# Seven products instead of eight for the gate projection of ten token tiles, in a one-core decoder layer

## The chip, the cores and the metric

One core of a Trainium2 chip runs the whole program. The metric is the device time of one execution in microseconds (us); the kernel was timed in three runs, and one further execution was recorded by the hardware profiler. The engines are named as in the profile: PE is TensorE (PEld its weight loads), DVE is VectorE, ACT is ScalarE, POOL is GpSimd, SP is SyncE, which here only issues DMAs.

## The reference

The program computes one decoder layer for x of 16 x 112 tokens by 1024, so 1792 rows. What matters here is its first part:

```python
s = silu(x @ w_gate.T)                     # 1792 x 2752
_, idx = top_k(-abs(s), 1376)              # per row: the 1376 smallest in size
s = s.at[rows, idx].set(0.0)
h = (s * (x @ w_up.T)) @ w_down.T          # 2752 -> 1024
x = layernorm(x + h)
```

Cross attention over a context of 16 x 375 rows (32 heads, 8 key heads), another layer norm and a 4-bit feed-forward layer follow. Everything in the part above is in float32.

## The kernel before

The 1792 rows are 14 tiles of 128 (`TT`), the 1024 inputs are 8 blocks of 128 (`KC`), the 2752 columns (`FF`) are cut in six chunks of 464 or 456 for the gate.

*One stream of matrix work.* `gates_up_keys` makes a queue, `stream`, of steps of TensorE work: the gate projection (`gate_chunk`, 14 tiles x 6 chunks), a step `swap` that closes the space of the gate's weights and opens the up projection's, the up projection (`up_unit`), and the keys and values of the context (`kv_unit`). `emit` takes the next step: it writes the step's matmuls, then the evacuation of the step before it from PSUM (`settle(1)`), then stores that are due (`issue`). Six PSUM banks (`ps_g`) hold products that wait for evacuation.

*A gate chunk* (L180 to L203) is 8 matmuls of 456 or 464 columns into one bank. Its evacuation is a sigmoid on ACT (L199), a multiplication with the bank on DVE (L200) and a store to `s_d` in DRAM by POOL's queue (L201).

*The up projection is already done by Strassen's seven products*, in Winograd's form: tiles are taken in pairs (two rows of blocks), the inputs and the columns in halves, and the columns in four passes (`UPASS`) of 344 (`UW`) out of each half. A unit is one pair in one pass: seven products of 4 matmuls of 344 columns (L297), named "A11 B11", "S2 T2", "A12 B21", "S1 T1", "S4 B22", "S3 T3", "A22 T4". S are sums of blocks of x, made once by POOL during the gate (`sums_of_x`, L175) and kept in DRAM (`xs_d`); T are sums of blocks of weights, made by POOL for each pass (`sum_weights`, L239, four operations). Of the seven evacuations two are copies on ACT (L315, L322), five are additions on DVE, and two results get a further addition on POOL (L325 for c12, L332 for u). Each of the four results is multiplied by the gate's s on POOL (L309) and stored by SP. x and its sums come by `load_first` (L245, L246) and `load_rest` (L252, L253), the weights by `load_weights` (L229).

*The search.* Beside the stream the 1376th smallest |s| of each row is found by bisection on the bits of a float. `load_row` brings a tile's row block from `s_d`, `start` takes the absolute value on ACT (L455), `count` counts the values below a candidate, 1824 columns on ACT (L468) and 928 on DVE (L471), and `update` sets the next candidate on DVE (L479, L480). A tile takes 31 counts. Two tiles run together: the first 16 counts of tile j take turns with the last 15 of tile j - 1. `finish` then queues pieces that build the mask: a count, two comparisons and four scans on DVE (L500, L511, L514, L518), then four pieces on POOL (L531, L532) and a store to `m_d`.

*What sets the order.* The order of instructions on every engine is the order in which the program writes them (`as_written`). The search writes a count, then calls `beside`, which writes one piece of `finish` and as much of the stream as is due:

```python
    share = sum(w for w, _ in list(stream)[:-ends]) / (2 * half * TT)
    def beside():
        nonlocal due
        due += share
        if pieces:
            pieces.popleft()()
        while due > 0 and len(stream) > ends:
            due -= emit()
```

A call of `beside` with the count before it is called a half-step here; there are 448 of them. The stream's steps weigh their columns (a chunk 456 or 464, a product 172, a key unit 285 or 404), so each half-step draws the same weight, 200. Search and stream are thus tied: each position of the search has one position of the stream. The search begins after 13 steps; the last 10 key units are kept for the end.

After this part come the masked products' transposes (between the key units), the down projection (L733), and attention with the last layer (L962 to L1181). They are not touched.

Of the kernel before, what the change touches and what calls it, by code (L numbers as in the profile page):

```python
# [56 lines left out]
LAG = 5  # L57
EARLY = 1
UNPACK = 4
PIECES = 4  # L60


# [44 lines left out]
def gates_up_keys(  # L107
# [50 lines left out]
    xts, acts = {}, {}  # L158

    def load_x(t):  # L160
        xts[t] = room(io, "e", f"xT_{t}", 4 * KH * P, KC, P, bufs=2)
        nc.sync.dma_start(xts[t], xT[t])

    def sums_of_x(j):

        a, b = xts.pop(2 * j), xts[2 * j + 1]
        s = []
        for x, y, op in (
            (b[:, :KH], b[:, KH:], ALU.add), (0, a[:, :KH], ALU.subtract),
            (a[:, :KH], b[:, :KH], ALU.subtract), (a[:, KH:], 1, ALU.subtract),  # L170
        ):
            i = len(s)
            s.append(room(io, "s", f"xs_{j}_{i}", 512, KH, P, bufs=5))
            x, y = (s[z] if isinstance(z, int) else z for z in (x, y))
            nc.gpsimd.tensor_tensor(s[i], x, y, op)  # L175
            nc.gpsimd.dma_start(xs_d[j][:, i], s[i])

    def gate_chunk(t, c):
        off, w = GATE_CHUNKS[c]
        if c == t % 2 and t + 1 < TT:  # L180
            load_x(t + 1)
        if c == 2 and t + 1 == TT:
            load_first(0)
        if c == 2 and t == 2:
            load_weights(0)
        if c == 2 and t == 6:
            sum_weights(0)
# [6 lines left out]
        if c == 0 and t % 2:  # L194
            sums_of_x(t // 2)

        def evacuate():
            s = io.tile([P, 512], F32, tag="s", name=f"s_{t}_{c}", bufs=5)
            nc.scalar.activation(s[:, :w], pg[:, :w], AF.Sigmoid)  # L199
            nc.vector.tensor_mul(s[:, :w], s[:, :w], pg[:, :w])  # L200
            nc.gpsimd.dma_start(s_d[t][:, ds(off, w)], s[:, :w])  # L201

        return evacuate  # L203


    stores = deque()

    def store_later(to, a):
        stores.append((len(stream), to, a))

    def issue(behind=2):
        while stores and stores[0][0] >= len(stream) + behind:
            nc.sync.dma_start(*stores.popleft()[1:])


    pairs = TT // 2
    n_up = UPASS * pairs
    w_up, first, rest, live = {}, {}, {}, {}

    def load_weights(p):  # L220

        if p % 2:
            u = room(upool[0], "w0", f"u0_{p}", 3 * KH * UW, 3, KH, UW)
            v = room(upool[0], "w1", f"u1_{p}", 4 * KH * UW, 4, KH, UW)
        else:
            u = room(lo, "lo0", f"u0_{p}", 5120, 3, KH, UW)
            v = room(lo, "lo1", f"u1_{p}", 5632, 4, KH, UW)
        for to, k, h in ((u[:, 0], 0, 0), (u[:, 2], 0, 1), (v[:, 0], 1, 0), (v[:, 1], 1, 1)):
            nc.sync.dma_start(to, wu[:, ts(k, KH), ds(h * FH + p * UW, UW)])  # L229
        w_up[p] = u, v  # L230

    def sum_weights(p):
        u, v = w_up[p]
        b11, t1, b12, b21, b22, t2, t4 = (
            z.rearrange("p k n -> p (k n)")
            for z in (u[:, 0], u[:, 1], u[:, 2], v[:, 0], v[:, 1], v[:, 2], v[:, 3])
        )
        for to, x, y in ((t1, b12, b11), (t2, b22, t1), (b12, b22, b12), (t4, b21, t2)):
            nc.gpsimd.tensor_tensor(to, x, y, ALU.subtract)  # L239

    def load_first(i):

        j = i % pairs
        a = first[i] = room(io, "e", f"xe_{i}", 4 * KH * P, 4, KH * P, bufs=2)
        nc.sync.dma_start(a[:, :2], xT[2 * j].rearrange("p (h k) n -> p h (k n)", h=2))  # L245
        nc.sync.dma_start(a[:, 2:], xs_d[j].rearrange("p h k n -> p h (k n)")[:, :2])  # L246

    def load_rest(i):

        j = i % pairs  # L250
        a = rest[i] = room(upool[0], "l", f"xl_{i}", 3 * KH * P, 3, KH * P, bufs=2)
        nc.sync.dma_start(a[:, :2], xs_d[j].rearrange("p h k n -> p h (k n)")[:, 2:])  # L252
        nc.sync.dma_start(a[:, 2], xT[2 * j + 1][:, KH:].rearrange("p k n -> p (k n)"))  # L253

    def side_loads(i):
        if i + 1 < n_up:
            load_first(i + 1)
            load_rest(i + 1)
        p, at = divmod(i, pairs)
        if at == (1 if p else 0) and p < UPASS - 1:  # L260
            load_weights(p + 1)
        if at == (4 if p else 2) and p < UPASS - 1:
            sum_weights(p + 1)
        if i == n_up - 4:
            load_keys()


    s_order = [(i, t, h) for i in range(n_up) for t, h in ((0, 0), (0, 1), (1, 0), (1, 1))]
    s_ahead = deque()

    def load_s():
        if s_order:
            i, t, h = s_order.pop(0)
            p, j = divmod(i, pairs)
            s = room(io, "s", f"us_{i}_{t}_{h}", 512, UW, bufs=5)
            nc.sync.dma_start(s, s_d[2 * j + t][:, ds(h * FH + p * UW, UW)])
            s_ahead.append((i, t, h, s))

    def up_unit(i, what):

        p, j = divmod(i, pairs)
        u, v = w_up[p]
        a, b, k = {
            "A11 B11": (first, 0, u[:, 0]), "A12 B21": (first, 1, v[:, 0]),
            "S1 T1": (first, 2, u[:, 1]), "S2 T2": (first, 3, v[:, 2]),
            "S3 T3": (rest, 0, u[:, 2]), "S4 B22": (rest, 1, v[:, 1]),
            "A22 T4": (rest, 2, v[:, 3]),
        }[what]
        st = live.setdefault(i, {})
        if what == "A11 B11":  # L290
            if i == 0:
                for _ in range(4):
                    load_s()
            side_loads(i)
        m = ps_g.tile([P, 512], F32, tag="pg", name=f"pu_{i}_{b}")[:, :UW]
        for n in range(KH):
            nc.tensor.matmul(  # L297
                m, a[i][:, b, ts(n, P)], k[:, n, :], start=(n == 0), stop=(n == KH - 1)
            )

        def own(tag):
            st[tag] = room(upool[0], tag, f"{tag}_{i}", 384, UW, bufs=3 if tag == "u" else 2)
            return st[tag]

        def store(t, h, tag):
            a = st.pop(tag)
            *of, s = s_ahead.popleft()
            assert of == [i, t, h]
            nc.gpsimd.tensor_tensor(a, a, s, ALU.mult)  # L309
            store_later(u_d[2 * j + t][:, ds(h * FH + p * UW, UW)], a)  # L310
            load_s()

        def evacuate():
            if what == "A11 B11":
                nc.scalar.copy(own("c11"), m)  # L315
            elif what == "S2 T2":
                nc.vector.tensor_add(own("u"), st["c11"], m)  # L317
            elif what == "A12 B21":
                nc.vector.tensor_add(st["c11"], st["c11"], m)
                store(0, 0, "c11")  # L320
            elif what == "S1 T1":
                nc.scalar.copy(own("m5"), m)  # L322
            elif what == "S4 B22":
                nc.vector.tensor_add(own("c12"), st["u"], m)
                nc.gpsimd.tensor_tensor(st["c12"], st["c12"], st["m5"], ALU.add)  # L325
                store(0, 1, "c12")
            elif what == "S3 T3":
                nc.vector.tensor_add(st["u"], st["u"], m)
            else:
                nc.vector.tensor_add(own("c21"), st["u"], m)  # L330
                store(1, 0, "c21")
                nc.gpsimd.tensor_tensor(st["u"], st["u"], st.pop("m5"), ALU.add)  # L332
                store(1, 1, "u")

        return evacuate
# [112 lines left out]
    state = {}  # L448

    def load_row(t):  # L450
        acts[t] = rows.tile([P, FF], F32, tag="a", name=f"a_{t}")
        nc.sync.dma_start(acts[t], s_d[t])

# [97 lines left out]
        load_rest(0)  # L551

    stream = deque()
    for t in range(TT):
        for c in range(len(GATE_CHUNKS)):
            stream.append((GATE_CHUNKS[c][1], lambda t=t, c=c: gate_chunk(t, c)))
    stream.append((0, swap))
    for i in range(n_up):
        for what in ("A11 B11", "S2 T2", "A12 B21", "S1 T1", "S4 B22", "S3 T3", "A22 T4"):
# [13 lines left out]
    def emit():  # L573
# [5 lines left out]
            issue()  # L579
        return w  # L580

    load_x(0)

    idle = ps_t.tile([P, 512], F32, tag="pt", name="idle")
# [927 lines left out]
```

## Time and profile before

| what | value |
| --- | --- |
| median of three runs | 2586.28 us (2581.89 to 2591.09) |
| the profiled execution, from first to last instruction | 2587.5 us |
| gate: first matmul to first matmul of the up projection | 6.2 to 528 us |
| up projection | 528 to 987 us |
| keys and values, with transposes | 987 to 1360 us |
| first count of the search, last count | 95.5 to 1312 us |
| mean TensorE clock granted | 0.990 |
| one count on ACT, on DVE | 1.815 us, 1.174 us |
| two passes of a gate matmul of 456 columns | 2 x 0.546 us, pipelined |

The trace records the execution from its first to its last instruction, and no time around it. A float32 matmul is recorded as two passes, so the counts of matmuls in the profile are twice those in the code. Matmuls are pipelined and their ends are modelled: the pace is read from the distance of starts, not from the duration. A bracket behind an instruction gives the idle time of its engine before it and what ended it. Stretches of the span are given in us from its start.

### The profile page before, as it was taken

How to read it: one execution, taken by the hardware profiler on the slowest of the kernel's cores; microseconds unless marked ns; L12 is line 12 of the kernel's file. 1: busy time of each engine (PE TensorE's matmuls, PEld its weight loads, DVE VectorE, ACT ScalarE, POOL GpSimd, SP SyncE). 2: the span in 40 equal slices, each digit the busy share in tenths (PEclk: the TensorE clock that was granted, in tenths of full speed). 3: DMA queues.
4: the chain of work that ended last, by engine and by line, in shares of the span. 5: the costliest groups of instructions: out<-in, count | busy, mean ns of one | idle time of the engine just before them, and what ended most of it. 6: DMA issues, size and time to landing. Idle time of an engine off the chain costs nothing.

```text
span 2587.5 us, 34811 instructions
## 1 busy us (share of the span) xinstructions
PE 2517.6 (97%) x10500; PEld 1527.3 (59%) x10514; DVE 1724.1 (67%) x3636; ACT 1390.3 (54%) x2470; POOL 1203.1 (46%) x1141
## 2 busy tenths in 40 slices
PE   9999999999999999999999999999989999999997
PEld 4444444466666666777764444444666666766663
DVE  0378788878988887677740343247667777777774
ACT  0487787777767776988830000000355555555553
POOL 1113433256457544454250000023478888878873
PEclk9999999999999999999999999999989999999999
DMA  6322332276768677888648223156687878778763
GB/s 244 133 69 87 109 106 76 96 263 231 240 231 278 227 243 268 290 288 292 223 160 289 87 82 112 57 188 225 173 201 184 204 191 202 193 191 193 196 168 110
DMA packets 283609, 478.65 MB, mean 185 GB/s; under 512 B 37856, under 2 KB 208224, under 8 KB 279328
## 3 DMA queue, kind: packets, MB, share of 16 engines
q1 hardware_dynamic: 241184, 374.06, 47.1%
q0 software_dynamic: 27008, 75.76, 9.5%
q10 hardware_dynamic: 15232, 26.62, 3.3%
q8 instruction: 85, 1.39, 0.2%
q14 instruction: 100, 0.82, 0.1%
HBM read 272.12 MB, written 103.50 MB: 145 GB/s over the span
## 4 chain that ended last, share of the span: by engine, by line
PE 49%; DVE 7%; DMA 5%; issue 3%; POOL 3%; ACT 3%; SPq 1%; ACTq 1%; POOLq 0%; DVEq 0%
PE m L733 14%; PE pu L297 7%; PE bank L1124 7%; PE bank L962 5%; PE pk L367 4%; PE pk L375 3%; PE sc L1032 3%; PE po L1087 3%; PE bank L1181 2%; ACT probs L1040 1%; DVE jv L471 1%; PE pt L439 1%; DVE nmax L1038 1%; DMA hm<-m_d 1%; DMA xr<-x_d 1%
## 5 line engine op out<-in xcount | busy, mean ns | idle before, releaser
L468 ACT ACTIVATE ja<-a,cand 128x1824 int8<-128x1824 f32 x434 | 787.9, 1815 | 195.1 <-DVE cand L480 187.0
L471 DVE TENSOR_SCALAR_CACHE_REDUCE jv<-a,cand 128x928 uint8<-128x928 f32 x434 | 509.7, 1174 | 43.6 <-ACT a L455 36.6
L190 PE MATMUL pg<-wg_sb,xT 128*128 128x456 f32 (+1 forms) x1344 | 519.3, 550 | 2.6 <-DMA wg_sb<-in_wg_dram 2.6
L190 PEld LDWEIGHTS pg<-wg_sb,xT 128*128 128x128 f32 x1344 | 255.8, 191 | 265.4 <-issue 257.8
L1040 ACT ACTIVATE probs<-sc,nmax 128x375 f32<-128x375 f32 x512 | 286.4, 572 | 230.7 <-DVE nmax L1038 213.2
L1049 POOL TENSOR_TENSOR probs<-probs,sums 128x1500 f32<-128x1500 f32 x128 | 344.2, 2689 | 129.1 <-DVE sums L1048 107.1
L1038 DVE TENSOR_REDUCE nmax<-sc 128x2 f32<-128x750 f32 x256 | 228.5, 931 | 132.3 <-PE sc L1032 132.2
L297 PE MATMUL pu<-u,xe 128*128 128x344 f32 x896 | 264.1, 453 | 2.3 <-DVE u L317 1.8
L733 PE MATMUL m<-wd,h 128*128 128x512 f32 (+1 forms) x616 | 266.2, 594 | 0.0
L1060 DVE STREAM_TRANSPOSE squares<-probs 128x1536 f32<-128x1536 f32 x128 | 224.1, 1751 | 23.7 <-DMA weights<-squares 13.6
L297 PEld LDWEIGHTS pu<-u,xe 128*128 128x128 f32 x896 | 170.0, 190 | 92.4 <-DVE u L317 2.9
L201 POOL DMA_DIRECT2D s_d<-s x84 | 45.9, 546 | 361.8 <-DVE s L200 298.1
L962 PE MATMUL bank<-x1T,wq_sb 128*128 128x224 f32 x1008 | 211.7, 364 | 0.0
L962 PEld LDWEIGHTS bank<-x1T,wq_sb 128*128 128x128 f32 x1008 | 189.3, 193 | 34.4 <-issue 30.7
L733 PEld LDWEIGHTS m<-wd,h 128*128 128x128 f32 (+1 forms) x616 | 117.2, 191 | 146.8 <-issue 144.8
L297 PE MATMUL pu<-u,xl 128*128 128x344 f32 x672 | 199.5, 453 | 1.9 <-DVE c L330 1.4
L1124 PE MATMUL bank<-wo_sb,aT 128*128 128x256 f32 x832 | 194.8, 388 | 0.0
L955 ACT COPY x1T<-pq 128x448 f32<-128x448 f32 x4 | 1.9, 535 | 349.1 <-DMA sc<-in_qs_dram 333.4
L1124 PEld LDWEIGHTS bank<-wo_sb,aT 128*128 128x128 f32 x832 | 155.3, 191 | 46.4 <-issue 23.8
L1074 POOL DMA_DIRECT2D weights<-squares x320 | 177.7, 561 | 6.9 <-PE po L1087 2.4
L421 POOL TENSOR_TENSOR hs<-hs,hm 128x512 f32<-128x512 f32 (+1 forms) x84 | 97.0, 1163 | 166.8 <-DMA hm<-m_d 148.8
L375 PE MATMUL pk<-wv_sb,ctx 128*128 128x256 f32 (+1 forms) x768 | 173.3, 379 | 0.0
(155 smaller groups left out, 3375.7 us busy)
## 6 DMA issues: line engine op xcount, KB each, us to landing
weights<-squares SPq DMA_DIRECT2D x704, 96.0 KB, 3.3
h<-hT_d SPq DMA_DIRECT2D x56, 640.0 KB, 4.9
weights<-squares POOLq DMA_DIRECT2D x320, 96.0 KB, 3.5
ctx<-in_ctxT_dram SPq DMA_DIRECT2D x16, 1500.0 KB, 8.5
a<-s_d SPq DMA_DIRECT2D x14, 1376.0 KB, 8.2
us<-s_d SPq DMA_DIRECT2D x112, 172.0 KB, 3.8
u_d<-c SPq DMA_DIRECT2D x84, 172.0 KB, 3.1
xe<-in_xT_dram SPq DMA_DIRECT2D x28, 512.0 KB, 5.4
```

The costliest lines, as they stand in the source:

```text
L190: nc.tensor.matmul(pg[:, :w], xts[t][:, kc, :], wg_sb[:, kc, ds(off, w)], start=(kc == 0), stop=(kc == KC - 1),)
L297: nc.tensor.matmul(m, a[i][:, b, ts(n, P)], k[:, n, :], start=(n == 0), stop=(n == KH - 1))
L375: nc.tensor.matmul(pk[:n, :KVD], c[:, kc, ds(at, n)], kv["v"][:, kc, :], start=(kc == 0), stop=(kc == KC - 1),)
L468: nc.scalar.activation(ja, a[:, NV:], AF.Sign, bias=cand, scale=-1.0, accum_out=st["sgn"])
L471: nc.vector.tensor_scalar(jv, a[:, :NV], cand, -(TOPK - 1 - NA / 2), ALU.is_lt, ALU.add, accum_out=st["nlt"])
L733: self.nc.tensor.matmul(bank, a[:r, k, :], b(k)[:r], start=(k == 0), stop=(k == HK - 1),)
L962: nc.tensor.matmul(pq[:, :GT], self.wq_sb[:, kc, ts(mc, P)], self.x1T[g][:, kc, :], start=(kc == 0), stop=(kc == KC - 1),)
L1038: nc.vector.tensor_reduce(nmax[h], sc[h][:, :, :SK], AX.X, ALU.max, negate=True)
L1040: nc.scalar.activation(pr[:, i, :SK], sc[i // 2][:, i % 2, :SK], AF.Exp, bias=nmax[i // 2][:, i % 2 : i % 2 + 1], accum_out=sums[:, i : i ...
L1049: nc.gpsimd.tensor_tensor(pr, pr, sums.unsqueeze(2).to_broadcast([P, 4, SK]), ALU.mult)
L1060: nc.vector.transpose(sq[:, :, n % 2].rearrange("p k (i f) -> p k i f", f=Q), probs[:, n % 3].rearrange("p i (k f) -> p k i f", f=Q),)
L1124: nc.tensor.matmul(pp[:, :256], aT[:, h, r, :], wo_sb[:, h * REP + r, ts(i, 256)], start=(h == 0 and r == 0), stop=(h == 1 and r == REP - 1),)
```

## The change

Tiles 0 to 3 keep the plain gate (24 chunks, `PLAIN = 4`). Tiles 4 to 13, five pairs, get their gate from the units of the up projection, with the gate's weights: the pairs come in two groups, (2, 3) and (4, 5, 6), and each group goes through four column passes. So there are 8 sets of gate weights (4 passes x 2 groups) and 20 gate units, then the 4 sets and 28 units of the up projection as before. Weights of a set are loaded and summed during the set before it.

- A gate unit's four results are not multiplied with s. They are queued (`unsaid`); at the next evacuation `silu` takes their sigmoid on ACT, multiplies on POOL and stores them to `s_d` by SP two steps later.
- x of all tiles is loaded during the first chunks: tiles 2 and 3 in a pair, tiles 4 to 13 at chunk 6 into the space that later holds weights. The sums of x of pairs 2 to 6 are made by POOL beside chunks 8, 10, 11, 12 and 13, of pairs 0 and 1 beside chunks 15 and 20. The first gate weights are loaded at chunk 14, once that space is free again, and summed at 18.
- A tile's row block is loaded for the search only when the tile's last result has been handed to its store (`whole`); until then `load_row` writes further steps of the stream.
- In the up projection, weights are loaded after the fourth product of the set's first unit and summed after the second product of its fourth unit (before: at the start of the second and of the fifth unit; for the first pass, of the first and third).
- `share` follows from the sum of the stream's weights, which is smaller: 192 instead of 200.

```diff
+PLAIN = 4
+GATE_PAIRS = ((2, 3), (4, 5, 6))
...
+    def load_others():
+
+        for tag, size, ts_ in (("lo0", 5120, (4, 5, 6, 7, 12)), ("lo1", 5632, (8, 9, 10, 11, 13))):
+            o = room(lo, tag, f"xo_{tag}", size, len(ts_), KC, P)
+            for i, t in enumerate(ts_):
+                xts[t] = o[:, i]
+                load_x(t)
...
+    beside_plain = {
+        0: lambda: load_x(1), 4: lambda: load_pair(1), 6: load_others, 8: lambda: sums_of_x(2), 10: lambda: sums_of_x(3),
+        11: lambda: sums_of_x(4), 12: lambda: sums_of_x(5), 13: lambda: sums_of_x(6),
+        14: lambda: load_weights(0), 15: lambda: sums_of_x(0), 18: lambda: sum_weights(0),
+        20: lambda: sums_of_x(1), 21: lambda: load_first(0),
+    }
...
+    sets = [(wg, p, js) for js in GATE_PAIRS for p in range(UPASS)]
+    sets += [(wu, p, tuple(range(pairs))) for p in range(UPASS)]
+    units = [(k, j) for k, (_, _, js) in enumerate(sets) for j in js]
...
+    def side_weights(i, b):
+
+        k, j = units[i]
+        if k + 1 == len(sets):
+            return
+        at, n = sets[k][2].index(j), len(sets[k][2])
+        if at == 0 and b == (2 if n < pairs else 3):
+            load_weights(k + 1)
+        if at == (1 if n < pairs else 3) and b == 1:
+            sum_weights(k + 1)
...
+    def silu():
+
+        while unsaid:
+            i, t, h, a = unsaid.popleft()
+            k, j = units[i]
+            g = room(io, "s", f"sg_{i}_{t}_{h}", 512, UW, bufs=5)
+            nc.scalar.activation(g, a, AF.Sigmoid)
+            nc.gpsimd.tensor_tensor(a, a, g, ALU.mult)
+            last = sets[k][1] == UPASS - 1 and (t, h) == (1, 1)
+            store_later(
+                s_d[2 * j + t][:, ds(h * FH + sets[k][1] * UW, UW)], a,
+                (2 * j, 2 * j + 1) if last else (),
+            )
...
         def store(t, h, tag):
             a = st.pop(tag)
+            if gate:
+                unsaid.append((i, t, h, a))
+                return
...
         def evacuate():
+            silu()
             if what == "A11 B11":
...
     def load_row(t):
+        while t not in whole:
+            emit()
...
-    for t in range(TT):
+    for t in range(PLAIN):
         for c in range(len(GATE_CHUNKS)):
             stream.append((GATE_CHUNKS[c][1], lambda t=t, c=c: gate_chunk(t, c)))
     stream.append((0, swap))
```

More of the change, by code (lines that the diff above doesn't have):

```diff
@@ L59 @@
 UNPACK = 4
+ORDER = ("A11 B11", "S2 T2", "A12 B21", "S1 T1", "S4 B22", "S3 T3", "A22 T4")
 PIECES = 4
@@ L160, in load_x, with load_pair @@
     def load_x(t):
-        xts[t] = room(io, "e", f"xT_{t}", 4 * KH * P, KC, P, bufs=2)
         nc.sync.dma_start(xts[t], xT[t])
+    def load_pair(j):
+        e = room(io, "e", f"xp_{j}", 4 * KH * P, 2, KC, P, bufs=2)
+        for i in range(2):
+            xts[2 * j + i] = e[:, i]
+            load_x(2 * j + i)
+    def load_others():
[4 more added lines that the diff above has]
+                load_x(t)
     def sums_of_x(j):
-        a, b = xts.pop(2 * j), xts[2 * j + 1]
+        a, b = xts[2 * j], xts[2 * j + 1]
         s = []
@@ L176, in sums_of_x @@
             nc.gpsimd.dma_start(xs_d[j][:, i], s[i])
+    beside_plain = {
[4 more added lines that the diff above has]
+    }
     def gate_chunk(t, c):
         off, w = GATE_CHUNKS[c]
[L180 to L187, printed above, removed]
         pg = ps_g.tile([P, 512], F32, tag="pg", name=f"pg_{t}_{c}")
@@ L193, in gate_chunk @@
             )
-        if c == 0 and t % 2:
-            sums_of_x(t // 2)
+        step = beside_plain.get(t * len(GATE_CHUNKS) + c)
+        if step:
+            step()
         def evacuate():
@@ L201, in evacuate, with store_later, load_weights, sum_weights @@
             nc.gpsimd.dma_start(s_d[t][:, ds(off, w)], s[:, :w])
+            if c == len(GATE_CHUNKS) - 1:
+                whole.add(t)
         return evacuate
     stores = deque()
-    def store_later(to, a):
-        stores.append((len(stream), to, a))
+    def store_later(to, a, ends=()):
+        stores.append((len(stream), to, a, ends))
     def issue(behind=2):
         while stores and stores[0][0] >= len(stream) + behind:
-            nc.sync.dma_start(*stores.popleft()[1:])
+            _, to, a, ends = stores.popleft()
+            nc.sync.dma_start(to, a)
+            whole.update(ends)
     pairs = TT // 2
[L217 to L224, printed above, removed]
-        else:
[L226 to L233, printed above, removed]
+    sets = [(wg, p, js) for js in GATE_PAIRS for p in range(UPASS)]
+    sets += [(wu, p, tuple(range(pairs))) for p in range(UPASS)]
+    units = [(k, j) for k, (_, _, js) in enumerate(sets) for j in js]
+    n_gate = sum(w is wg for w, _, js in sets for _ in js)
+    n_up = len(units)
+    wts, first, rest, live = {}, {}, {}, {}
+    whole, unsaid = set(), deque()
+    def load_weights(k):
+        w, p, _ = sets[k]
+        if k % 2:
+            u = room(upool[0], "w0", f"u0_{k}", 3 * KH * UW, 3, KH, UW)
+            v = room(upool[0], "w1", f"u1_{k}", 4 * KH * UW, 4, KH, UW)
+        else:
+            u = room(lo, "lo0", f"u0_{k}", 5120, 3, KH, UW)
+            v = room(lo, "lo1", f"u1_{k}", 5632, 4, KH, UW)
+        for to, i, h in ((u[:, 0], 0, 0), (u[:, 2], 0, 1), (v[:, 0], 1, 0), (v[:, 1], 1, 1)):
+            nc.sync.dma_start(to, w[:, ts(i, KH), ds(h * FH + p * UW, UW)])
+        wts[k] = u, v
+    def sum_weights(k):
+        u, v = wts[k]
         b11, t1, b12, b21, b22, t2, t4 = (
@@ L241, in load_first @@
     def load_first(i):
-        j = i % pairs
+        j = units[i][1]
         a = first[i] = room(io, "e", f"xe_{i}", 4 * KH * P, 4, KH * P, bufs=2)
@@ L248, in load_rest @@
     def load_rest(i):
-        j = i % pairs
+        j = units[i][1]
         a = rest[i] = room(upool[0], "l", f"xl_{i}", 3 * KH * P, 3, KH * P, bufs=2)
@@ L258, in side_loads @@
             load_rest(i + 1)
[L259 to L263, printed above, removed]
         if i == n_up - 4:
             load_keys()
-    s_order = [(i, t, h) for i in range(n_up) for t, h in ((0, 0), (0, 1), (1, 0), (1, 1))]
+    def side_weights(i, b):
[7 more added lines that the diff above has]
+            sum_weights(k + 1)
+    s_order = [(i, t, h) for i in range(n_gate, n_up) for t, h in ((0, 0), (0, 1), (1, 0), (1, 1))]
     s_ahead = deque()
@@ L273, in load_s @@
             i, t, h = s_order.pop(0)
-            p, j = divmod(i, pairs)
+            k, j = units[i]
             s = room(io, "s", f"us_{i}_{t}_{h}", 512, UW, bufs=5)
-            nc.sync.dma_start(s, s_d[2 * j + t][:, ds(h * FH + p * UW, UW)])
+            nc.sync.dma_start(s, s_d[2 * j + t][:, ds(h * FH + sets[k][1] * UW, UW)])
             s_ahead.append((i, t, h, s))
+    def silu():
+        while unsaid:
+            i, t, h, a = unsaid.popleft()
+            k, j = units[i]
+            g = room(io, "s", f"sg_{i}_{t}_{h}", 512, UW, bufs=5)
[6 more added lines that the diff above has]
+            )
     def up_unit(i, what):
-        p, j = divmod(i, pairs)
-        u, v = w_up[p]
-        a, b, k = {
+        k, j = units[i]
+        p, gate = sets[k][1], i < n_gate
+        u, v = wts[k]
+        a, b, w = {
             "A11 B11": (first, 0, u[:, 0]), "A12 B21": (first, 1, v[:, 0]),
@@ L290, in up_unit @@
         if what == "A11 B11":
-            if i == 0:
+            if i == n_gate:
                 for _ in range(4):
@@ L294, in up_unit @@
             side_loads(i)
-        m = ps_g.tile([P, 512], F32, tag="pg", name=f"pu_{i}_{b}")[:, :UW]
+        m = ps_g.tile([P, 512], F32, tag="pg", name=f"pu_{i}_{what[:2]}_{b}")[:, :UW]
         for n in range(KH):
             nc.tensor.matmul(
-                m, a[i][:, b, ts(n, P)], k[:, n, :], start=(n == 0), stop=(n == KH - 1)
+                m, a[i][:, b, ts(n, P)], w[:, n, :], start=(n == 0), stop=(n == KH - 1)
             )
+        side_weights(i, ORDER.index(what))
         def own(tag):
@@ L558, in gates_up_keys @@
     for i in range(n_up):
-        for what in ("A11 B11", "S2 T2", "A12 B21", "S1 T1", "S4 B22", "S3 T3", "A22 T4"):
+        for what in ORDER:
             stream.append((UW / 2, lambda i=i, what=what: up_unit(i, what)))
@@ L580, in emit @@
         return w
+    pair = room(io, "e", "xp_0", 4 * KH * P, 2, KC, P, bufs=2)
+    xts[0], xts[1] = pair[:, 0], pair[:, 1]
     load_x(0)
```

## The prediction

> **What bounds the kernel now.** I read the page's engine table first, then busy time by stretch, then ScalarE's and GpSimd's order of time inside a stretch.
>
> ```profile
> PE 2517.6 (97%) x10500; PEld 1527.3 (59%) x10514; DVE 1724.1 (67%) x3636; ACT 1390.3 (54%) x2470; POOL 1203.1 (46%) x1141
> ```
>
> By the page TensorE is the bound and any matmul saved is time saved. The stretches (columns: length, then busy PE, PEld, DVE, ACT, POOL) say something narrower. The first is the gate beside the search, the second the up projection beside it, the third the keys.
>
> ```profile
> 93.00:528.00 435.00, 435.00 (x1133) 214.86 (x1132) 345.56 (x929) 343.32 (x394) 142.65 (x155) 1.00 0.26 94
> 528.00:987.00 459.00, 454.78 (x1569) 297.14 (x1568) 392.84 (x1050) 343.29 (x392) 259.17 (x228) 1.00 0.74 248
> 987.00:1260.00 273.00, 266.93 (x1164) 198.48 (x1163) 198.01 (x527) 231.43 (x333) 120.96 (x109) 0.99 0.88 289
> ```
>
> PE is full, but DVE and ACT are at 75 to 86%, and their work, the search, is a loop between them: a count on ACT (L468) and DVE (L471), then the new candidate (L480). Inside the up stretch ACT's list shows how little it is short of full:
>
> ```profile
> 577.58 1.82 ACT L468 ACTIVATE ja<-a,cand 128x1824 int8<-128x1824 f32 x1 [1.27 <-DVE cand L480]
> 580.67 1.81 ACT L468 ACTIVATE ja<-a,cand 128x1824 int8<-128x1824 f32 x1 [1.18 <-DVE cand L480]
> ...
> 612.84 1.82 ACT L468 ACTIVATE ja<-a,cand 128x1824 int8<-128x1824 f32 x1
> 614.56 0.19 ACT L468 ACTIVATION_READ_ACCUMULATOR ja<-a,cand 128x1 f32 x1
> 614.78 1.82 ACT L468 ACTIVATE ja<-a,cand 128x1824 int8<-128x1824 f32 x1
> 616.50 0.19 ACT L468 ACTIVATION_READ_ACCUMULATOR ja<-a,cand 128x1 f32 x1
> 616.59 0.42 ACT L315 COPY c<-pu 128x344 f32<-128x344 f32 x1
> 616.92 1.82 ACT L468 ACTIVATE ja<-a,cand 128x1824 int8<-128x1824 f32 x1
> ```
>
> At 612 to 617 nothing is in brackets: counts follow each other every 1.94 us and a copy puts 0.33 between them. There ACT is the bound, not PE. At 577 to 581 ACT waits for DVE, which runs the finishing pieces of the last tile. PE is full throughout because its six PSUM banks let it run up to five products ahead. So **both sides are the bound**, within a few per cent, and PE's 97% hides the second one.
>
> What the search needs by itself, per tile, from this list: 4.5 us at the start (L455 at 563.24 to the second count at 567.71), nine half-steps with finishing pieces in 32.8 (567.71 to 600.54), and 21 half-steps of 1.94 plus copies. In the up stretch that is 4.5 + 32.8 + 21 x 2.05 = 80.3 us, with the waits on GpSimd seen there about 83; PE's share of one tile was 87. (Starts of L455: 563.2, 648.1, 736.6, 819.7, 909.1, so 86.5 on average.) In the key stretch the starts are 88 to 90 apart, and ACT hardly pauses.
>
> **The change, part by part.**
>
> *TensorE.* Removed: 60 chunks. 83 of them took 527.6 - 15.3, so 6.17 us each, 370 us. Added: 20 units of seven products. 28 units had 454.8 us of PE in the up stretch, 16.24 each, so 325 us. PE alone: **-45 us**.
>
> *Search per unit of program order.* The stream's weight falls (60 x 459 columns become 140 x 172), so a half-step draws 192 instead of 200 of it, 1.12 products. The ten tiles' gate spans 24080/192.2 = 125 half-steps, 121 counts, 3.9 tiles of search.
>
> *ScalarE and VectorE there.* A gate chunk cost ACT 0.44 (171.13 to 171.57) and held DVE. A gate unit costs two copies (0.33 each, from the list) and four sigmoids of 344 columns, not in the trace: between the copy of 344 (0.33) and the sigmoid of 464 (0.44); I take 0.34. That is 2.0 us per unit, 0.34 per half-step. Where ACT is the bound a half-step is then 1.94 + 0.34 = 2.28. Over the 125 half-steps: the rest of the second tile of search, 22 counts, 50; three whole tiles at 4.5 + 32.8 + 21 x 2.28 = 85.2, 256; the first quarter of the next, with its finishing pieces, 29. Sum **335 us**, against 325 of PE. So the search becomes the bound of this stretch, by 10 us, before any new wait.
>
> *The new wait.* In a gate unit ACT takes the sigmoid of c12 and of u after GpSimd's addition to them. Before, ACT waited for GpSimd only to get a buffer back; now every count queued on ACT behind such a sigmoid waits with it, then DVE's L479, then the search. GpSimd works in order, and this is what it does beside a sum of weights (L239):
>
> ```profile
> 558.70 3.10 POOL L239 TENSOR_TENSOR u<-u 128x1376 f32<-128x1376 f32 x1
> 561.88 6.18 POOL L239 TENSOR_TENSOR u<-u,u 128x1376 f32<-128x1376 f32 x2
> 568.01 3.11 POOL L239 TENSOR_TENSOR u<-u 128x1376 f32<-128x1376 f32 x1
> 571.09 0.90 POOL L309 TENSOR_TENSOR c<-c,us 128x344 f32<-128x344 f32 x1
> 571.96 0.90 POOL L332 TENSOR_TENSOR u<-u,m 128x344 f32<-128x344 f32 x1
> ```
>
> 12.4 us in one block, and what is queued comes after. The change sums weights eight times in the stretch (three times before, in the up stretch). From the block's start to the addition to c12 there are 12.4 + 4 x 0.9 and the 1.4 before it, 17.4; ACT reaches the sigmoid six products later, 6 x 2.28/1.12 = 12.2. Wait: 5 us, or none where finishing pieces stretch a half-step to 3.6. I count five of eight blocks outside such pieces: 23 us. The four masks of a tile (L531, L532, 3.0 us each) do the same: 609.8 to 626.5 in the trace they hold GpSimd some 6 us behind, two dependent sigmoids fall in it, 3 tiles x 3 = 9. **32 us.** Bounds: nothing (ACT's copies beside masks and sums waited at most 2.9 in the up stretch, so the order may spare them), and eight whole blocks, 99. I take 32, since it follows from the order of the queue.
>
> A side cost of more GpSimd work: a product of GpSimd (L309) that ran beside a VectorE scan took 2.1 instead of 0.91 us, and the scan 1.85 instead of 1.64 (589.0 and 588.5 us); 3 of 28 products of u met one. For three tiles I price that at 1 us, inside the rounding. The Trainium skill, "GPSIMD Engine Reference", section Specifications, says more: the two engines share their SBUF interfaces and contend when VectorE has two SBUF inputs or a 2-port mode. An estimate by that rule slows all 26 finishing pieces of the stretch by the row's 0.21, 5 us on top of the sum.
>
> *DMA.* In the first group a set serves two units, 32.5 us: weights 2.8 MB, x and sums 3.6, stores 1.4, rows 0.8; 8.6 MB or 263 GB/s, beside 248 in the up stretch and 300 in the key stretch. Weights landed 11.0 us after issue, 14.5 at most; GpSimd comes to sum them six products (14 us) later at the least. Hidden by that; if late, GpSimd stands and the 32 grows. Between -5 and +10: nothing.
>
> *Queues and order.* 60 stores leave GpSimd's queue (0.55 each, 33 us) and 80 go to SP's (0.32 to 0.43, 30 us), where SP no longer waits for x; they wait for GpSimd's products, as the up stretch's stores did. New is that a row is asked for only when its tile is whole: tile 4 is whole 20640 columns into the stream, and the search asks at 26000. Nothing; without that lead whole units would go ahead of counts, 16 us each.
>
> *Start.* SP's loads of x (L162) were stuck until 85.5 and the first row behind them; now x has its own space, so the row lands early and the first Abs moves from 93.0 to about 87.5, where ACT's evacuation of chunk 11 ends. But five sums of x stand on GpSimd in chunks 8 to 13, each 8.6 us (43.96 to 52.56) beside chunks of 6.17, and use the five buffers that the chunks store from: about 3 us back. SP stands at the first weights until GpSimd is done, near 102; behind it is the second row, wanted at 136. The draw being smaller, the plain stretch ends at 163 on the search's clock, as before. Nothing.
>
> **The sum on the search's clock.** Ten tiles' gate: 163 + 335 + 32 = 530 (before 527). Up: PE starts five banks early, 518 + 455 = 973; the search needs 5.48 tiles, 451 us with 3 of waits each, so 981; I take 983 (before 987). Keys: the search has 0.15 of a tile more left to do than before, 0.285 x 86 + 2 x 86 + 129 = 325.5; PE 14 x 22.7 = 318; they are near enough to cost 2 more: 1310.5 at the last count, before 1312.6. Everything after follows unchanged: -2, and -8 if PE and the search never hinder each other. I take **-5**: 2587.5 - 5 = 2582.5 against the profiled span. The trace holds nothing around the span; the median of the runs is 1.2 lower, so 2581.
>
> **Rivals.** (1) *GpSimd's waits are hidden*: half or none of the 32. Then -5 - 16 to -5 - 32, 2565 to 2549; about 2556. For: the 2.9 above, and additions that start ahead of their half-step. Against: GpSimd at 87% in the first group (12.4 + 11 + 5 of 32.5). (2) *GpSimd sets the pace of the first groups*, the side where it is slower: each block meets masks or late weights, and waits double to 64. Then -5 + 32, 2613; about 2606. Place: the sigmoid of c12 and u; price: 4 us more per block; it decides from 40 us of waits on. For: masks and sums meet in two of the three tiles. (3) *The stretch is PE's after all*, full -45: 2541; the counts without a pause at 612 to 617 speak against it.
>
> **How the numbers follow.** About 0.3%, 8 us, can be told from no change. Forecast 0.40 (own range 2568 to 2596); rival 1 with 3, 0.33; rival 2 0.27. Faster: 0.33 + 0.10; slower: 0.27 + 0.06; same 0.24. The range reaches to 2552 and 2612.
>
> **What would show it.** PE's idle in the ten tiles' gate: 35 to 45 us, where the old gate had none. ACT's largest new wait: on GpSimd's additions, 25 to 40 us in all. Starts of Abs 93 to 96 apart in the third to fifth tile, then 83 to 86. The first Abs near 87.5. If Abs starts are 84 apart in the gate, rival 1 holds; if 100, rival 2. Wrong in kind: PE waiting for x or weights from DMA, or the up stretch losing what the gate won.

## The result, and the profile after

The changed kernel takes 2611.4 us (median of four runs, 2609.0 to 2612.3), beside 2587.5 (now also four runs) for the kernel before: ratio 1.0095, 95% interval 1.0073 to 1.0117. It is **slower by 24 us**, where I had forecast 5 us faster. The time lies outside the forecast's own range (2568 to 2596), at the upper edge of the range that took the rivals in (2552 to 2612). The place is that of the second rival: the sigmoids of c12 and u, which stand behind GpSimd. Line numbers move: after, a gate unit's products are L345, its copies L368 and L375, its sigmoid L318 and product L319, GpSimd's additions L378 (c12) and L385 (u), the sums of weights L266, the counts L523 and L526, the scans L573.

The engine table of the profile after, to be held against the first line of the prediction:

```profile
PE 2490.0 (96%) x10660; PEld 1560.0 (60%) x10674; DVE 1737.8 (67%) x3676; ACT 1411.2 (54%) x2530; POOL 1386.0 (53%) x1233
```

TensorE is busy for 28 us less and the span is 20 us longer, so TensorE now stands still for part of the time. GpSimd is busy for 183 us more. Busy time by stretch, after (length, then busy PE, PEld, DVE, ACT, POOL): the gate beside the search, up to TensorE's first matmul of the up projection; the up projection, up to the first matmul of the keys; the keys:

```profile
87.00:535.20 448.20, 406.62 (x1302) 248.76 (x1300) 336.71 (x892) 336.72 (x424) 297.14 (x220) 0.98 0.60 210
535.20:1004.60 469.40, 459.10 (x1568) 297.61 (x1569) 408.77 (x1103) 360.54 (x413) 269.42 (x234) 1.00 0.69 237
1004.60:1278.00 273.40, 261.03 (x1131) 193.44 (x1130) 200.91 (x528) 230.99 (x330) 118.89 (x111) 0.99 0.87 288
```

In the gate, PE stands for 42 of 448 us, where it stood for none before, and the up projection begins 7 us later than before (535.2 against 528.0) instead of 10 us earlier. The up projection then takes 469 us for 459, and PE stands for 10 of them. The granted clock in the gate is 0.98 for 1.00; with 42 us to spare there TensorE doesn't set the pace, so that isn't the cause. ScalarE's waits for GpSimd in the gate's units (waited for: us in total, times, longest) point to it:

```profile
ACT sg L318 <- POOL c L378: 53.9, 15, 9.0
ACT sg L318 <- POOL u L385: 4.6, 7, 1.1
```

That is 58.5 us against the 32 of my sum. The largest of these waits, first on GpSimd:

```profile
260.06 3.11 POOL L266 TENSOR_TENSOR u<-u 128x1376 f32<-128x1376 f32 x1
263.25 6.19 POOL L266 TENSOR_TENSOR u<-u,u 128x1376 f32<-128x1376 f32 x2
269.40 3.10 POOL L266 TENSOR_TENSOR u<-u 128x1376 f32<-128x1376 f32 x1
...
275.08 1.48 POOL L586 TENSOR_TENSOR e<-e,c 128x688 bf16<-128x688 bf16 x1
276.64 1.49 POOL L587 TENSOR_TENSOR m<-m,e 128x688 bf16<-128x688 bf16 x1
278.08 0.91 POOL L378 TENSOR_TENSOR c<-c,m 128x344 f32<-128x344 f32 x1
```

and on ScalarE at the same time:

```profile
268.08 1.82 ACT L523 ACTIVATE ja<-a,cand 128x1824 int8<-128x1824 f32 x1
269.80 0.19 ACT L523 ACTIVATION_READ_ACCUMULATOR ja<-a,cand 128x1 f32 x1
279.03 0.49 ACT L318 ACTIVATE sg<-c 128x344 f32<-128x344 f32 x1 [9.04 <-POOL c L378]
279.42 1.80 ACT L523 ACTIVATE ja<-a,cand 128x1824 int8<-128x1824 f32 x1
```

The addition to c12 comes at 278.08, behind a block of sums, three products and a mask; the sigmoid waits for it, and the next count waits behind the sigmoid. For 9 us ScalarE counts nothing.

The search's own clock is the start of Abs, the absolute value with which a tile's search begins (first start, distances, last start, in us; all from the order of ScalarE's instructions). The gate's units lie beside the end of the second to the start of the sixth distance; the third to fifth are theirs alone.

| kernel | 1st | distances 1 to 7 | 14th |
| --- | --- | --- | --- |
| before | 93.0 | 48.7, 74.9, 86.5, 84.3, 86.3, 89.5, 84.9 | 1182.1 |
| after | 87.4 | 55.6, 77.9, **101.5, 97.8, 95.6**, 82.5, 88.1 | 1211.5 |
| no_sums | 89.1 | 55.6, 72.2, 87.8, 87.3, 89.9, 82.5, 87.2 | 1175.0 |
| fill_sums | 89.0 | 55.6, 77.6, 100.9, 92.4, 95.7, 82.5, 87.4 | 1203.2 |
| keep_sums | 87.3 | 55.7, 78.4, 97.6, 87.3, 89.8, 82.5, 87.4 | 1191.6 |
| kept_late_spaced | 87.6 | 55.8, 73.7, 96.7, 83.1, 83.5, 86.9, 85.2 | 1173.8 |

Against before, the search after is 4 us late at the third tile, 42 at the sixth, 29 at the last. The last count ends 27 us later than before (1339.6 against 1312.3), the profiled execution 20.

### The profile page after: what moved, and what is told of

It is laid out like the page before. It is cut to its first block, busy times and chain, and to the rows that moved or that the text cites. A ratio compares the mean times of both kernels' runs of the same rounds, so it can differ in the third digit from the quotient of the medians.

```text
span 2607.2 us, 35719 instructions
## 1 busy us (share of the span) xinstructions
PE 2490.0 (96%) x10660; PEld 1560.0 (60%) x10674; DVE 1737.8 (67%) x3676; ACT 1411.2 (54%) x2530; POOL 1386.0 (53%) x1233
## 4 chain that ended last, share of the span: by engine, by line
PE 57%; DVE 15%; DMA 7%; POOL 7%; ACT 6%; issue 6%; SPq 1%; POOLq 0%; ACTq 0%; DVEq 0%
PE m L790 18%; PE bank L1181 7%; PE pu_S L345 6%; PE pg L206 5%; PE bank L1019 5%; PE pu_A L345 5%; DVE jv L526 4%; PE sc L1089 3%; ACT ja L523 3%; PE po L1144 3%; DVE c L573 3%; POOL u L266 2%; DMA a<-s_d 2%; PE bank L1238 1%; DVE m L555 1%
## 5 line engine op out<-in xcount | busy, mean ns | idle before, releaser
L523 ACT ACTIVATE ja<-a,cand 128x1824 int8<-128x1824 f32 x434 | 788.2, 1816 | 152.1 <-DVE cand L535 145.4
L526 DVE TENSOR_SCALAR_CACHE_REDUCE jv<-a,cand 128x928 uint8<-128x928 f32 x434 | 509.5, 1174 | 46.1 <-ACT a L510 40.1
L345 PE MATMUL pu_A<-u,xe 128*128 128x344 f32 x768 | 241.5, 458 | 13.1 <-DVE u L370 11.5
L345 PE MATMUL pu_S<-u,xe 128*128 128x344 f32 x768 | 239.6, 455 | 12.3 <-DVE c L377 10.3
L345 PE MATMUL pu_S<-u,xl 128*128 128x344 f32 x768 | 234.0, 456 | 15.2 <-DVE u L381 7.1
L345 PEld LDWEIGHTS pu_S<-u,xl 128*128 128x128 f32 x768 | 145.5, 191 | 97.2 <-DVE u L381 11.5
L345 PEld LDWEIGHTS pu_A<-u,xe 128*128 128x128 f32 x768 | 146.8, 192 | 93.6 <-DVE u L370 15.4
L345 PEld LDWEIGHTS pu_S<-u,xe 128*128 128x128 f32 x768 | 145.5, 191 | 92.7 <-DVE c L377 14.5
L920 POOL TENSOR_TENSOR y<-y,c 128x512 f32<-128x512 f32 x7 | 9.9, 1420 | 324.5 <-DMA zi<-in_qz_dram 324.3
```

What stands on the lines that cost most here:

```text
L345: nc.tensor.matmul(m, a[i][:, b, ts(n, P)], w[:, n, :], start=(n == 0), stop=(n == KH - 1))
L523: nc.scalar.activation(ja, a[:, NV:], AF.Sign, bias=cand, scale=-1.0, accum_out=st["sgn"])
L526: nc.vector.tensor_scalar(jv, a[:, :NV], cand, -(TOPK - 1 - NA / 2), ALU.is_lt, ALU.add, accum_out=st["nlt"])
```

## The experiments

The expectations name four theories. A: ScalarE stands behind GpSimd's queue, and the blocks of sums make the queue. B: the sigmoids' own time on ScalarE is the cost, and the waits only show it. C: GpSimd has too much to do, or its reading holds VectorE back. D: TensorE itself is slower than counted. Each row is a median and its ratio to the kernel before on the same chip. The last column is taken from the 2611.4 us of the changed kernel; the runs are from several chips, on which the kernel before took 2584.8 to 2587.5 us, so differences of 3 us in that column say nothing.

| run | median us | ratio, 95% interval | against after |
| --- | --- | --- | --- |
| short_before | 2572.8 | 0.9945 (0.9901 to 0.9989) | |
| short_after | 2528.7 | 0.9771 (0.9743 to 0.9799) | |
| dve_adds | 2594.9 | 1.0042 (1.0027 to 1.0056) | -16.5 |
| late_silu | 2595.0 | 1.0041 (1.0028 to 1.0054) | -16.4 |
| no_sums | 2575.0 | 0.9962 (0.9947 to 0.9977) | -36.4 |
| no_silu | 2564.2 | 0.9925 (0.9902 to 0.9949) | -47.2 |
| spread_sums | 2600.9 | 1.0063 (1.0047 to 1.0080) | -10.5 |
| spread_late | 2599.4 | 1.0061 (1.0045 to 1.0077) | -12.0 |
| keep_sums | 2592.5 | 1.0032 (1.0018 to 1.0047) | -18.9 |
| keep_spread_late | 2581.8 | 0.9994 (0.9976 to 1.0012) | -29.6 |
| fill_sums | 2602.9 | 1.0069 (1.0056 to 1.0083) | -8.5 |
| spaced_masks | 2609.6 | 1.0098 (1.0083 to 1.0114) | -1.8 |
| kept_late_spaced | 2576.7 | 0.9965 (0.9953 to 0.9977) | -34.7 |

**TensorE's saving: short_before, short_after.** The same edit in both kernels cuts the search's counts to 64 columns on each engine:

```diff
-ja, a[:, NV:], AF.Sign
+ja[:, :64], a[:, NV : NV + 64], AF.Sign
-jv, a[:, :NV], cand, -(TOPK - 1 - NA / 2)
+jv[:, :64], a[:, :64], cand, -31.0
```

> The kernel before with the search's counts cut to 64 columns on each engine (so the output is not the reference's); every instruction and its order stay. TensorE is then the only bound: 2570 to 2588 if its 97% was the truth, and PE without idle in the gate and up stretches.

> The changed kernel with the same cut. All theories on the search (A, B, C): 40 to 48 below the cut kernel before, since TensorE's 45 us of saving is then all that differs, less a few us where it waits for GpSimd's sums of weights. Rival D (transfers or sums of weights hold TensorE itself): less than 25 below.

With the counts cut short the change gains 44.1 us (2572.8 - 2528.7). TensorE's 45 are real, and theory D falls; with full counts they can't be collected, because the search sets the pace. For the kernel before, short counts gain only 14 us (2586.4 to 2572.8).

**The additions on VectorE: dve_adds.**

```diff
-nc.gpsimd.tensor_tensor(st["c12"], st["c12"], st["m5"], ALU.add)
+(nc.vector if gate else nc.gpsimd).tensor_tensor(st["c12"], st["c12"], st["m5"], ALU.add)
```

(and the addition to u likewise)

> In the gate units the additions to c12 and to u go from GpSimd to VectorE; nothing else moves. Theory A (every search count on ScalarE queues behind a sigmoid that waits for GpSimd's addition): ScalarE's waits on GpSimd, 58 us in the changed kernel, fall to under 10; VectorE pays 40 x 0.45 = 18 us, of which about 7 in half-steps with finishing pieces count. Abs starts 88 to 92 apart in the third to fifth tile (changed kernel: 101, 98, 96), time 2611 - 25 to 2611 - 40, so 2571 to 2586. Rival B (the sigmoids' own time on ScalarE and the search's tie are the cost, the waits only show it): under -8. Rival C (GpSimd has too much to do, or slows VectorE at the shared memory): -5 to -15, since only 37 of its 230 us in the stretch go.

ScalarE's waits for c12 and u were gone, yet only 16.5 us came back, less than theory A asked for. VectorE got the additions, 32 of them between 220 and 515 us with 34.7 us in all, and one looked like this (VectorE, in order of time):

```profile
290.12 0.50 DVE L383 TENSOR_TENSOR c<-u,pu_A 128x344 f32<-128x344 f32 x1
290.65 5.09 DVE L385 TENSOR_TENSOR u<-u,m 128x344 f32<-128x344 f32 x1
295.67 1.17 DVE L526 TENSOR_SCALAR_CACHE_REDUCE jv<-a,cand 128x928 uint8<-128x928 f32 x1
```

The addition of 344 elements takes 5.09 us while GpSimd multiplies and then sums weights; half of them took 0.52 to 0.58, so the 32 would have needed about 17 us undisturbed. The one ahead of it, with one input in PSUM, takes 0.50 as ever. Moving the work to the neighbour costs the neighbour twice its own time.

**The sigmoids later: late_silu.** The sigmoid and product are written three evacuations after their sum instead of one.

```diff
-        while unsaid:
+        while unsaid and (
+            unsaid[0][0] == n_gate - 1 or unsaid[0][4] >= len(stream) + 3
+        ):
```

> Same instructions, but each sigmoid and product of a gate unit is written three evacuations after its value instead of one. Theory A: GpSimd has some 4 us more before ScalarE asks; waits of 5 us go to 1, of 9 to 5: 58 us become 10 to 20, Abs starts 87 to 91 apart, time 2571 to 2585. Rivals B and C: no work is saved, so within 5 us of 2611.

The time, 2595.0, lies between what A and what B and C asked for. ScalarE's waits on the addition to c12 fell to 21.8, and VectorE got new ones, here from its waits between 157 and 540 us:

```profile
DVE u L372 <- POOL c L321: 15.7, 4, 5.5
...
DVE u L372 <- DMA s_d<-u: 5.7, 2, 3.5
```

The u buffers stay taken until GpSimd has multiplied and the result is stored: part of the wait was turned into another one.

**No sums, no sigmoids: no_sums, no_silu.** no_sums leaves out the sums of the gate's weights (its products read the plain blocks); no_silu leaves out the gate units' sigmoid and multiplication.

```diff
     def sum_weights(k):
+        if sets[k][0] is wg:
+            return
```

> The sums of the gate's weights are left out (gate products that need them take raw blocks instead, so the output is not the reference's). GpSimd loses nine blocks of 12.4 us. Theory A: the waits left are those beside masks, 10 to 20 of 58 us; time 2611 - 25 to -38. Rival B: under -8. Rival C (GpSimd's load): more than moving the additions brings, since 112 us of GpSimd go, -30 to -45.

> Sigmoid and product of the gate units are left out, the sums are stored as they are (output not the reference's). Theory A: waits (58) and the sigmoids' own 80 x 0.38 = 30 us both go from ScalarE; the stretch becomes TensorE's, its 20 units 325 us plus little; time 2611 - 55 to -70, so 2541 to 2556, about the 45 below before that TensorE alone promised. The difference to the version with the additions on VectorE is the price of ScalarE's added work: 20 to 30. Rival B: nearly all of the difference is here and not in the other runs, too. Rival D (TensorE itself is slower than counted, by loads of x or weights): stays above 2575.

The eight blocks of sums (the expectation says nine) cost 36.4 us, as theory A had it, and as C had it too; B, with less than 8, falls. Without sigmoids 47.2 go, where A asked for 55 to 70: nothing then stands behind GpSimd between ScalarE's counts, and PE is busy for 336 of the 343 us from 157 to 500. ScalarE's waits that are left without sums:

```profile
ACT sg L320 <- POOL c L382: 25.5, 11, 4.4
ACT sg L320 <- POOL u L389: 4.6, 7, 1.1
```

**The sums cut up: spread_sums, spread_late.**

```diff
+        if k and b == 1 and sets[k][2][0] == j:
+            sum_weights(k, (3,))
...
-        if at == (1 if n < pairs else 3) and b == 1:
-            sum_weights(k + 1)
+        if at == (1 if n < pairs else 3) and b in (1, 2, 3):
+            sum_weights(k + 1, (b - 1,))
```

> All of the change and the same work; only the four operations of a set's weight sums are no longer one block of 12.4 us on GpSimd: three are queued one product apart (second, third and fourth product of the unit), the fourth in the second product of the next unit, when the additions to c12 are past. Theory A (the blocks cost because ScalarE's sigmoids stand behind them): ScalarE's waits on GpSimd fall from 58 to 15 to 30 us and the time falls by 20 to 30, to 2581 to 2591. Theory C (the blocks cost because VectorE is slowed while GpSimd sums, however the sums are cut up): the waits fall as much, the finishing pieces of VectorE stay as long as after the change, and the time falls by under 12, to 2599 to 2611.

> The spread sums and, beside them, each sigmoid and product two evacuations after its sum instead of one. Same work. Theory A: ScalarE hardly waits for GpSimd (under 12 us) and the time is 2565 to 2580, below both kernels. Theory C: the waits go and the time stays near the 2595 that later sigmoids alone gave, 2588 to 2598.

Both miss what theory A asked for; the time of spread_sums is the one that C gave. There ScalarE's waits on the addition to c12 fell only from 53.9 to 39.9: three operations of 3.1 us, one product apart, still queue in front of other work. And VectorE's scans beside the gate's units were held no less than in the changed kernel: four of the 16 took 2.48 to 4.06 us instead of about 1.6, and with later sigmoids four took 2.91 to 4.23. Later sigmoids took the waits on c12 down to 26.2 and the time by nothing clear; where that went wasn't tried.

**The second group's sums from HBM: keep_sums, keep_spread_late.** The first group stores its sums, the second loads them.

```diff
+        kept = w is wg and k >= UPASS
...
+        if kept:
+            for q, to in enumerate((u[:, 1], v[:, 2], u[:, 2], v[:, 3])):
+                nc.sync.dma_start(to, t_d[p][:, q])
...
+        if k < UPASS and at == 0 and b == 6:
+            keep_sums(k)
...
-        if at == (1 if n < pairs else 3) and b == 1:
+        if at == (1 if n < pairs else 3) and b == 1 and not UPASS <= k + 1 < 2 * UPASS:
             sum_weights(k + 1)
```

> All of the change, but the first group writes its sums of the gate's weights to HBM and the second group loads them (seven loads per set instead of four, 4.9 MB instead of 2.8), so four of the eight blocks of sums in the stretch are gone and the other four stay whole. Same result computed. Leaving out all blocks took 36 us off; half of that is 18, so both theories say 2590 to 2596. If the larger loads come late, TensorE shows waits for DMA on its products in the second group, and the time is 2600 or more.

> Kept sums for the second group, spread sums in the first, sigmoids two evacuations later. Theory A: the waits are as good as gone already by spreading, so keeping adds little: 2560 to 2577, and within 8 us of the spread sums with later sigmoids. Theory C: keeping takes half of VectorE's slowing away, so 10 to 20 us below the spread sums with later sigmoids: 2572 to 2585.

Half of the blocks gone, half of the 36 us gone. The table of Abs shows it by place: the third distance, beside the first group, stays at 97.6; the next two are 87.3 and 89.8. The larger loads (284 GB/s between 157 and 540 us, 216 after the change) weren't late: none of PE's waits names them. keep_spread_late came out 17.6 us below spread_late, as theory C had it.

**Waiting and holding told apart: fill_sums.** As no_sums, but GpSimd writes zeros where it summed.

```diff
+        if sets[k][0] is wg:
+            for a, n in ((u[:, 1], 3), (v[:, 2], 2), (v[:, 3], 2), (u[:, 1], 3)):
+                for _ in range(n):
+                    nc.gpsimd.memset(a, 0.0)
+            return
```

> The gate weights' sums are left out (so the output is not the reference's), and where each of them stood GpSimd writes zeros ten times over 1376 elements of the places that no product reads: it should be held for about as long (an estimate of 10 to 13 us from 0.31 us for 256 elements), but it reads nothing. Without any block 36.4 us were gone; by the traces I put 28 of them down to ScalarE standing behind the blocks and 8 to 9 to VectorE's pieces being held while GpSimd sums. By that account ScalarE's waits on GpSimd's additions come back (from 30 to 50 to 60 us) and the time is 2598 to 2606, with VectorE's scans at their undisturbed 1.65 us; if writing alone holds VectorE as well, 2606 to 2614 with scans of 2 us and more. Rival: the waits are mostly hidden beside the finishing pieces and VectorE's holding makes the 36: then the time stays at 2575 to 2585 when the scans are undisturbed.

The length of the block came out right, 12.6 us, and so did the time, 2602.9. The same place in both kernels, first the scans and the block of the changed kernel:

```profile
338.91 4.06 DVE L573 TENSOR_TENSOR_SCAN c<-unit,e 128x688 uint16<-128x688 bf16 x1
344.40 2.90 DVE L573 TENSOR_TENSOR_SCAN c<-unit,c,e 128x688 uint16<-128x688 bf16 x1
349.15 2.48 DVE L573 TENSOR_TENSOR_SCAN c<-unit,c,e 128x688 uint16<-128x688 bf16 x1
```

```profile
338.41 3.10 POOL L266 TENSOR_TENSOR u<-u 128x1376 f32<-128x1376 f32 x1
341.59 8.59 POOL L266 TENSOR_TENSOR u<-u,u 128x1376 f32<-128x1376 f32 x2
350.14 4.39 POOL L266 TENSOR_TENSOR u<-u 128x1376 f32<-128x1376 f32 x1
```

then, with zeros in the block's place (VectorE's and GpSimd's lists of fill_sums):

```profile
339.62 1.58 DVE L580 TENSOR_TENSOR_SCAN c<-unit,e 128x688 uint16<-128x688 bf16 x1
342.64 1.64 DVE L580 TENSOR_TENSOR_SCAN c<-unit,c,e 128x688 uint16<-128x688 bf16 x1
346.14 1.64 DVE L580 TENSOR_TENSOR_SCAN c<-unit,c,e 128x688 uint16<-128x688 bf16 x1
```

```profile
339.11 12.61 POOL L264 MEMSET u<- 128x1376 f32 x10
```

When GpSimd only writes, these scans keep their time; when it reads two tensors, scan and sum slow each other: the block takes 16.1 us for 12.4 and the scans up to 4.06 for 1.6. In the changed kernel only this one of the eight blocks met a tile's scans; the others took 12.4 us. The times then split the 36.4: from no_sums to fill_sums 27.9 us, in which ScalarE's waits on the two additions rose from 30.1 to 61.6; from fill_sums to after 8.5 us, in which the waits did not rise. The second figure is loose: the ratios, each against the kernel before on its own chip, give 6.7 us with intervals that overlap, and the profiles give 4.5 us, by which the up projection's first matmul moved (501.2 us in no_sums, 530.7 in fill_sums, 535.2 after). **Some 28 us are waiting, 5 to 8 are holding.** Both theories hold, A for three quarters or more.

**The rest: spaced_masks.**

```diff
-        pieces.extend(lambda i=i: mask(i) for i in range(PIECES))
+        for i in range(PIECES):
+            pieces.extend([lambda i=i: mask(i), lambda: None])
```

> All of the change, and the four masks of a tile, which stand on GpSimd one half-step after another (3.0 us each in half-steps of 2.3), are put every second half-step. Same work. Without any sums ScalarE still waited 30 us for GpSimd's additions, most of it beside masks. If the masks' queue makes those waits, they fall by 10 to 20 us and the time by 6 to 14, to 2597 to 2605. Rival: the additions come late by their own chain (VectorE's addition, then GpSimd's, then the sigmoid) whatever else stands in the queue: no change, 2607 to 2613.

No change: the wait of 4.5 us behind the last masks went (490.77 in after, 489.39 here), others grew, and the sum is 57.4 for 58.5. So the masks are not what most of the remaining 30 us wait for. no_sums shows what is (VectorE's, GpSimd's and ScalarE's instructions in one list):

```profile
334.86 0.94 DVE L586 TENSOR_SCALAR c<-c,left 128x2752 bf16<-128x2752 uint16 x1
335.71 0.50 DVE L381 TENSOR_TENSOR c<-u,pu_S 128x344 f32<-128x344 f32 x1
...
336.35 0.91 POOL L382 TENSOR_TENSOR c<-c,m 128x344 f32<-128x344 f32 x1 [4.80 <-issue]
...
337.29 0.49 ACT L320 ACTIVATE sg<-c 128x344 f32<-128x344 f32 x1 [3.72 <-POOL c L382]
```

GpSimd had been idle for 4.80 us (the view names no releaser; VectorE's addition, which it needs, ends just before). The sum of c12 itself is late, behind a finishing piece on VectorE, and the sigmoid, one step of the stream later, is already due: half-steps take 1.12 products on average, so some take two, and then no count lies between. Of the eleven waits three have masks in front (2.8, 1.1 and 4.4 us), one a block of the up projection (4.2), the other seven this bare chain: 13 us. These are lengths of waits; what this chain costs in time no run tried by itself.

**Together: kept_late_spaced** (the edits of keep_spread_late and spaced_masks).

> Kept sums for the second group, spread sums in the first, sigmoids two evacuations later, and masks every second half-step. Same result computed. The three without the spaced masks were level with the kernel before. If masks still hold the additions up there (24 us of waits were left), 6 to 14 us less: 2568 to 2576, faster than both kernels; if the chain is late by itself, 2579 to 2585, level again.

2576.7 us, ratio 0.9965: faster than both kernels, by 35 us than the change and 9 than before, and between the two forecasts. Its gate distances after the first group are 83.1 and 83.5. Its step from keep_spread_late, 5 us, is about the size of the two intervals, so what the spaced masks give there is open.

## Why the prediction was wrong

TensorE's term was right, and so was summing on the search's clock. What failed is the term **"32 us"** of waits on GpSimd in the gate's units, and with it the choice between forecast and second rival: the waits were 58.5 us, and the chain that ScalarE waits for with nothing queued in front had been put at nothing. The miss by place, in us of the profiled execution:

| | before | forecast | after | no_sums |
| --- | --- | --- | --- | --- |
| first matmul of the up projection | 528.0 | 518 | 535.2 | 501.2 |
| first matmul of the keys | 987.2 | 983 | 1004.6 | 969.4 |
| end of the last count | 1312.3 | 1310.5 | 1339.6 | 1303.0 |

The kernel is 17 us later than forecast at the end of the gate, and 12 more are lost behind it. In the gate, leaving out the blocks of sums gives back 34.0 us, where the forecast had 23 of waits and 1 of holding: 10 of the 17. The other 7 lie in what is named below; no run divides them.

1. *TensorE -45:* right, 44.1 with short counts.
2. *The search becomes the bound:* right. PE idle 35 to 45 was forecast, 42 came. First Abs "near 87.5": 87.4.
3. *Waits, 23 for blocks:* of the eight blocks that the sum counts (seven of the gate's weights, one of the up projection's) seven made a wait, of 4.2 to 9.0 us, 39.0 in all; the sum had five of 5 us (which make 25 and not 23). That the waits behind the gate's blocks cost their length is shown: 28 us by fill_sums.
4. *Waits, 9 for masks:* two waits, 5.5 us. What the sum lacked is the **bare chain**: VectorE's addition, GpSimd's addition, sigmoid, with nothing queued in front. I had bounded the wait from below by copies that waited at most 2.9 us, and took what is behind a queue for the whole of it. It is 9.4 us at c12 and 4.6 at u by the trace. With the other two that makes the 58.5 where 32 stood.
5. *VectorE beside GpSimd, 1 us by the rows:* 5 to 8. The rows were of products of 344 elements, and six of the 28 products of u took 2.1 us, where I had counted three; the change put a sum of 1376 beside the scans. The Trainium skill, "GPSIMD Engine Reference", section Specifications, says that VectorE's instructions with two SBUF inputs contend with GpSimd. The scans of up to 4.06 us agree with it. The estimate of 5 us that went by it came near by luck: it slowed 26 pieces by 0.21 us each, and what slowed were four scans beside one block, by 5.4 in all. The skill's "VectorE: DVE Perf Modes", section "Two Vector instructions with no wait between them", names the second SBUF *read* interface as the one shared. fill_sums agrees, with scans of 1.58 to 1.64 beside a GpSimd that only writes.
6. *Sigmoid 0.34 us:* 0.38 from start to start (185.04, 185.42), 3 us over 80.
7. *Start, net nothing:* the first distance is 55.6 for 48.7, with 12.9 us of ScalarE's waits for the store buffers in it, so the early first Abs (5.6 us) was used up and 1 more. At the third Abs the search is 4 us late; the other 3 are those of a first block, since no_sums is there as early as before (216.8 against 216.6).
8. *DMA and queues, nothing:* right in the gate. In the up stretch rows came late for three tiles (7.0, 3.1, 5.6 us); ScalarE waits 16.2 for rows in all, 9.8 before.

Of the 12 us behind the gate, 9 are also lost in no_sums, so they are not the blocks' doing; its rows come late by 14 us as well. That late rows make the loss fits, but wasn't tried by itself. The forecast of 983 also had a slip: 5.48 tiles at 83 us are 455 and not 451. From the last count to the end the kernel regains 7 us on the kernel before; why is open. So the profiled execution ends 24.7 us above the 2582.5 of my sum (2607.2).

The second rival gave the time well (2606), with 64 us of waits, but not by its own mechanism: weights were never late (GpSimd waits for none in the gate's units), and only one wait, the one of 9.0, had both a block and a mask in front. Its number is in part luck.

The change does take 44 us from TensorE. With full counts none of it reaches the time: the search, with the sigmoids added to ScalarE, is the bound already, and ScalarE's new dependence on GpSimd makes it slower than before.

## What to carry to other kernels

When two sides bind within a few per cent, work taken from one is worth only the gap, and what the change adds to the other can cost more than that. Before an in-order engine inside a saturated loop is made to wait for another engine, add up the chain it waits for with empty queues first, then the queues. Here no single remedy brought the kernel below the one before: halving the sums gave back 19 us, moving the additions or delaying the sigmoids 16 each, spreading the sums 10. Only a combination with half of the sums kept reached it.

## What the runs showed of the hardware

- GpSimd's two-input sums and VectorE's instructions with two SBUF inputs hold each other: a scan of 688 elements took 2.48 to 4.06 us for 1.6, an addition of 344 took up to 5.09 (dve_adds) for 0.52, and the block of sums 16.1 for 12.4. VectorE's additions with one input in PSUM (0.48 beside the sums, 0.50 elsewhere) and its counts with one input (1.15 to 1.17) did not change.
- A zero-fill by GpSimd of 12.6 us, in the same place, left the scans at 1.58 to 1.64 us.
- A sigmoid of 344 columns took 0.47 to 0.49 us, and 0.38 from start to start; a copy of as many, 0.42 and 0.33.
